# A graph layer on one core: edges turned by VectorE in blocks of 32x32, own rows fetched in four transfers

## The chip, the cores and the metric

One core of a Trainium2 chip runs the whole layer in one launch. The metric is the device time of one execution in microseconds; three executions of the kernel before gave 17,978.58, 17,993.09 and 18,013.70 us, a median of 17,993.09 us. The engines of the core work side by side, each through its own list of instructions in order: PE (TensorE), DVE (VectorE), ACT (ScalarE), POOL (GpSimd) and SP (SyncE, which here only starts transfers). They wait for one another through semaphores.

## The reference

50,000 nodes have 160 features each: 64 scalars and 32 vectors of three. There are 1,650,000 edges, sorted by their target `dst`; 50,000 of them lead from a node to itself. Each edge has four numbers.

```python
s, v = x[:, :64], x[:, 64:].reshape(n, 32, 3)
ss, vv = s[src], v[src]
e0, e1 = sh[:, 0:1], sh[:, 1:4]
dot = einsum('eui,ei->eu', vv, e1)
out0 = C0 * (ss * e0 @ W1 + dot * INV3 @ W2)
p3 = (ss @ W3)[:, :, None] * e1[:, None, :] * INV3
p4 = einsum('eui,uw->ewi', vv * e0[:, :, None], W4) * INV3
p5 = einsum('eui,uw->ewi', cross(vv, e1[:, None, :]), W5) * INV6
m = concatenate([out0, (C1 * (p3 + p4 + p5)).reshape(-1, 96)], axis=1)
m_agg = segment_sum(m, dst, n)
h = (m_agg times Ws and Wv)
x = layernorm(x + (x + relu(h)))
```

The messages are linear in x[src] and in the four numbers of the edge. So the kernel sums, for each node and each of the four numbers k, `attr[e, k] * x[src[e]]` over the node's edges, and applies one matrix of 4 x 160 rows by 160 columns, made of all weights, to each node afterwards.

## The kernel before

**Units.** 128 edges are a unit, 6 units (768 edges) a group, 2 groups a pair, 20 groups (10 pairs) a load. There are 2,087 groups, 1,044 pairs and 105 loads. As edges are sorted, the targets of a group lie within 32 consecutive nodes (`W`).

**A pair.** For each of its 12 units POOL starts one indirect transfer (`gather`, L349): 128 rows of x, picked by the indices in `si`, go to `xg`. There are four buffers of `xg`, so POOL may be 4 x 12 gathers ahead of PE. VectorE makes the weights of the sums (`spread`): `hot` (L358) marks which of 32 nodes each edge belongs to, `ha` (L361) multiplies it by the four numbers in `pk`. PE multiplies `ha` by `xg`, unit by unit, into `ps` (L386; each product is two weight loads and two matmuls in the profile). VectorE turns `ps` in blocks of 32x32 (L398, `turn_sums`) and adds each group's result to `ring` at the group's place (L405). The ring holds 768 nodes; a segment is 512 nodes, and at a segment's first group the part that reached past the last segment is carried over (L402). The order in VectorE's and PE's lists is that of the main loop: in pair p, after the second product `turn_sums` of pair p-1 is emitted, after the fourth `spread` of pair p+1, and tasks from a queue are worked off in between.

**Blocks.** When the last group that can touch a block of 128 nodes has been summed (`last_of`), its block is due: 391 in all, 2 or 3 pairs apart. Two pairs later PE multiplies the ring by the matrix (L704, `phb`), then VectorE adds x (y, L182, which waits for `phb`), makes the statistics and the normed row, and SP sends it out.

**Placing a load.** SP loads 120 units with a unit on each partition. `place`, four pairs later, turns them so that an edge lies on each partition: a product with a matrix of ones (L320) spreads each group's first target, from `first` (L318) to `baseB` (L322); PE transposes sources and targets into PSUM (L326, L327) and the four numbers into `pk` (L331); VectorE makes the indices `si` (L334) and the offsets `rel` (L337). `aim` turns the groups' first targets into places in the ring.

**Own edges.** All edges behind the first 76,800 are first packed (`pack`): VectorE takes the edges from a node to itself out of rows of 790 edges, SP writes the rest to `edges` and the four numbers of the own edges to `selves`, both in DRAM, by two transfers for each of 1,994 rows. Loads behind the first five read from `edges`, 24 bytes an edge. The own edges' share is put in when a segment begins: `ask_own`, six pairs ahead, loads x of 256 nodes to all four quarters of the partitions (`xr`, 640 KB) and the shares (`sr`, single numbers); `set_own`, two pairs ahead, multiplies them (L689) and turns the product into the ring (L693).

SP's list holds all loads and stores in the order of emission; a transfer that must wait holds those behind it.

Of the kernel before, what the change touches and what calls it, by code (L numbers as in the profile page):

```python
# [39 lines left out]
F32 = mybir.dt.float32  # L40
I32 = mybir.dt.int32
# [3 lines left out]
ALU = mybir.AluOpType  # L45
# [57 lines left out]
def tile_gnn_resnorm(ctx: ExitStack, tc: tile.TileContext, x, src, dst, attr, W1, W2, W3, W4, W5, Ws, Wv, out, n_edges):  # L103
# [123 lines left out]
    with tc.tile_pool(name="once", bufs=1) as once, tc.tile_pool(name="raw", bufs=2) as rawp, \  # L227
# [17 lines left out]
        nc.vector.tensor_copy(slotsP, slots)  # L245

# [3 lines left out]
        def load(s):  # L250

            g0 = s * SG
            n = (min(NG, g0 + SG) - g0) * G
            if g0 >= NH:
                p0 = g0 * G * P - EH
                r6 = rawp.tile([P, P, 2 + NK], F32, name="r6")
                dq.dma_start(r6[:n].rearrange("u p c -> u (p c)"),
                             edges[0, p0 * (2 + NK):(p0 + n * P) * (2 + NK)].rearrange("(u q) -> u q", u=n))
                return s, n, None, r6[:n, :, 0], r6[:n, :, 1], r6[:n, :, 2:]
            e = slice(g0 * G * P, (g0 * G + n) * P)  # L260
            ri = rawp.tile([P, 2, P], I32, name="ri")
            ra = rawp.tile([P, P, NK], F32, name="ra")
            dq.dma_start(ri[:n, 0, :], src1[e].rearrange("(u p) o -> u (p o)", p=P))
            dq.dma_start(ri[:n, 1, :], dst1[e].rearrange("(u p) o -> u (p o)", p=P))
            dq.dma_start(ra[:n].rearrange("u p k -> u (p k)"), attr[e].rearrange("(u p) k -> u (p k)", p=P))
            return s, n, ri, None, None, ra[:n]

        def cast(loaded):
            s, n, ri, sf, df, af = loaded
            if ri is not None:  # L270
                rf = rawp.tile([P, 2, P], F32, name="rf")
                begun.append(nc.scalar.copy(rf[:n], ri[:n]))
                sf, df = rf[:n, 0, :], rf[:n, 1, :]
            return s, n, sf, df, af
# [37 lines left out]
        def place(cast_):  # L312

            s, n, sf, df, af = cast_
            ng = n // G

            first = idxp.tile([P, SG], F32, name="first")
            nc.vector.tensor_scalar(first[:n], starts[:n], df[:, 0:1], None, op0=ALU.mult)  # L318
            yield 1
            nc.tensor.matmul(bank[:, 3, :ng], ones[:n], first[:n, :ng], start=True, stop=True)  # L320
            baseB = idxp.tile([P, SG], F32, name="baseB")
            nc.vector.tensor_scalar(baseB[:, :ng], bank[:, 3, :ng], float(N - 1), None, op0=ALU.min)  # L322
            aim(s, ng, baseB)
            yield 1
            pi = bank[:, 1:3, :]
            nc.tensor.transpose(pi[:, 0, :n], sf, ident[:n, :n])  # L326
            nc.tensor.transpose(pi[:, 1, :n], df, ident[:n, :n])  # L327
            yield 1.5
            pk = psK.tile([P, NK, P], F32, name="pk")
            for k in range(NK):  # L330
                begun.append(nc.tensor.transpose(pk[:, k, :n], af[:, :, k], ident[:n, :n]))  # L331
                yield 0.75
            si = idxp.tile([P, P], I32, name="si")
            nc.vector.tensor_scalar(si[:, :n], pi[:, 0, :n], 0.0, float(N - 1), op0=ALU.max, op1=ALU.min)  # L334
            rel = idxp.tile([P, P], F32, name="rel")

            nc.vector.scalar_tensor_tensor(  # L337
                rel[:, :n].rearrange("p (g j) -> p g j", j=G), pi[:, 1, :n].rearrange("p (g j) -> p g j", j=G),
                float(N - 1), baseB[:, :ng].unsqueeze(2).to_broadcast([P, ng, G]),
                op0=ALU.min, op1=ALU.subtract)  # L340
            nc.vector.tensor_reduce(extremes[:, 0, s:s + 1], rel[:, :n], axis=AX.X, op=ALU.min)
            begun.append(nc.vector.tensor_reduce(extremes[:, 1, s:s + 1], rel[:, :n], axis=AX.X, op=ALU.max))
            placed[s] = si, rel, pk
# [50 lines left out]
        def turn_sums(p, ps):  # L394

            s, g, ng = pairs[p]
            at = sump.tile([P, PG, ND, W], F32, name="sums")
            nc.vector.transpose(at[:, :ng], ps[:, :ng].rearrange("p g (b f) -> p g b f", f=FB))  # L398
            for i in range(ng):
                k = seg_of[g + i]  # L400
                if k and g + i == first_of[k]:
                    nc.vector.tensor_tensor(ring[k][:, :, :TW - S], ring[k][:, :, :TW - S], ring[k - 1][:, :, S:],  # L402
                                            op=ALU.add)
                here = ring[k][:, :, ds(find(g + i), W)]
                nc.vector.tensor_tensor(here, here, at[:, i], op=ALU.add)  # L405
# [255 lines left out]
        def ask_own(k, bs, got):  # L661
# [7 lines left out]
            xr = ownp.tile([P, BP * P // W, D], F32, name="xr")  # L669
            sr = ownp.tile([P, BP * P // W], F32, name="sr")  # L670
            xs = x[n0:n1, :].rearrange("(w q) d -> w (q d)", q=nq).unsqueeze(0).to_broadcast([NK, m, nq * D])
            ss = selves[0, n0 * NK:n1 * NK].rearrange("(w q k) -> k w q", q=nq, k=NK)
            with nc.allow_non_contiguous_dma(reason="one number of each node"):
                if m == W:
                    dq.dma_start(xr[:, :nq].rearrange("p q d -> p (q d)"), xs)
                    dq.dma_start(sr[:, :nq], ss)
                else:
                    nc.vector.memset(xr[:, :nq], 0.0)
                    nc.vector.memset(sr[:, :nq], 0.0)
                    for k_ in range(NK):  # L680
                        r = slice(k_ * W, k_ * W + m)
                        dq.dma_start(xr[r, :nq].rearrange("p q d -> p (q d)"), xs[k_])
                        dq.dma_start(sr[r, :nq], ss[k_])
            got.extend((xr, sr, nq))

        def set_own(k, bs, got):

            xr, sr, nq = got
            nc.vector.tensor_tensor(xr[:, :nq], xr[:, :nq], sr[:, :nq].unsqueeze(2).to_broadcast([P, nq, D]), op=ALU.mult)  # L689
# [25 lines left out]
        starts = once.tile([P, SG], F32, name="starts")  # L715
        nc.gpsimd.iota(starts, pattern=[[G, SG]], base=0, channel_multiplier=-1, allow_small_or_imprecise_dtypes=True)
        nc.vector.tensor_scalar(starts, starts, 0.0, None, op0=ALU.is_equal)
# [9 lines left out]
        nc.vector.memset(limit, float(KM))  # L727
        none = once.tile([P, 1], I32, name="none")
# [98 lines left out]

        packs, due = [], []
        for i in range(npacks):

            first = next(s for s in range(NH // SG, NSC)
                         if min(NG, (s + 1) * SG) * G * P - EH > row_start(i * RP)[0][0])
            own = next((k for k in range(NSEG) if min((k + 1) * S, N) > row_start(i * RP)[1][0] and own_blocks(k)), NSEG - 1)
            due.append(min((first - 1) * per - 1, first_of[own] // PG - 7))
# [4 lines left out]
        for k in range(1, NSEG):  # L839
            p = first_of[k] // PG  # L840
            after_pair(max(p - 3, START), begin_segment, k)
            for bs in own_blocks(k):
                got = []
                after_pair(p - 6, ask_own, k, bs, got)
# [8 lines left out]
        for p, (s, g, ng) in enumerate(pairs):  # L853
            if p % per == 0 and s + 1 < NSC:
                end = min(NG, (s + 2) * SG) * G * P - EH
# [200 lines left out]
```

## Time and profile before

| what | value |
|---|---|
| median of three executions | 17,993.09 us |
| the profiled execution | 18,022.17 us |
| its span, first to last instruction | 18,020.0 us |
| mean granted clock of TensorE | 0.625 |
| POOL busy | 12,137.8 us (67%) |
| DVE busy | 7,032.6 us (39%) |
| PE busy | 6,879.0 us (38%) |
| DMA queue of POOL, share of 16 engines | 23.7% |
| DMA queue of SP, share of 16 engines | 6.1% |

A row of the page's groups reads: line, engine, operation, what it writes and reads, how often; then busy time in us and the mean of one in ns; then how long the engine was idle just before such instructions, and what ended most of that. "issue" means that the engine waited for nothing that the profile shows, "remote" that a semaphore ended the wait whose sender the profile can't name. A row of waits reads: who waited, for whom, us in total, how many times, the longest. A row of the timeline reads: start in us, duration in us, engine, line, operation, and in brackets the idle time before.

### The profile page before, as it was taken

The numbers are of one execution on the slowest core, as the hardware profiler recorded it, in microseconds if no ns is written. First come the engines' busy times: TensorE is split into PE (matmuls) and PEld (weight loads), VectorE is DVE, ScalarE is ACT, GpSimd is POOL, SyncE is SP. The second block draws the span as 40 slices with busy tenths as digits, with TensorE's granted clock in tenths as the row PEclk, the third lists the DMA queues.
The fourth block names the chain that finished last, engine by engine and source line by source line (L and its number), as shares of the span: only waits on it lengthen the run. The fifth ranks groups of instructions, "written<-read, shape, count | busy, mean of one in ns | idle before, by whom it ended". The sixth has DMA issues, their size and how long they took to land. (4 is left out here: it accounts for less than half of the span.)

```text
span 18020.0 us, 99721 instructions
## 1 busy us (share of the span) xinstructions
PE 6879.0 (38%) x29811; PEld 6014.7 (33%) x29812; DVE 7032.6 (39%) x11269; ACT 227.8 (1%) x479; POOL 12137.8 (67%) x12535
## 2 busy tenths in 40 slices
PE   3333334343333333333333333334333333333333
PEld 3333333333333333333333333333333333333333
DVE  4343443434434343443433434344343433434332
ACT  0000000000000000000000000000000000000000
POOL 6666666666666666666666666666666666666666
PEclk6666666666666666666666666666666666666666
DMA  2222323232232322323223232322323223232222
GB/s 71 74 69 72 80 71 81 69 82 72 73 79 70 83 71 73 79 69 81 72 72 79 70 79 72 82 69 72 80 70 82 69 73 80 69 79 72 73 72 63
DMA packets 961715, 1337.18 MB, mean 74 GB/s; under 512 B 411739, under 2 KB 716048, under 8 KB 957182
## 3 DMA queue, kind: packets, MB, share of 16 engines
q0 software_dynamic: 601056, 1026.60, 23.7%
q1 hardware_dynamic: 358674, 302.87, 6.1%
q8 instruction: 238, 3.90, 0.1%
q14 instruction: 307, 2.51, 0.0%
q10 hardware_dynamic: 1440, 1.29, 0.0%
HBM read 1258.50 MB, written 71.40 MB: 74 GB/s over the span
## 5 line engine op out<-in xcount | busy, mean ns | idle before, releaser
L349 POOL DMA_INDIRECT xg<-in_x,si x12522 | 12134.1, 969 | 5859.5 <-issue 3666.1
L386 PE MATMUL ps<-xg,ha 128*128 128x160 f32 x25044 | 6255.4, 383 | 9081.8 <-issue 8146.9
L386 PEld LDWEIGHTS ps<-xg,ha 128*128 128x128 f32 x25044 | 5171.1, 254 | 9859.0 <-issue 8902.6
L398 DVE STREAM_TRANSPOSE sums<-ps 128x320 f32<-128x320 f32 x1044 | 529.7, 507 | 6341.5 <-remote 4050.5
L361 DVE TENSOR_TENSOR ha<-hot,pk 128x1536 f32<-128x1536 f32 x1044 | 1830.2, 1753 | 35.8
L182 DVE SCALAR_TENSOR_TENSOR y<-phb,xt 128x160 f32<-128x160 f32 x391 | 125.6, 321 | 3508.3 <-PE ps L386 1623.2
L704 PE MATMUL phb<-BWk,ring 128*128 128x160 f32 (+1 forms) x3910 | 1181.7, 388 | 454.0 <-issue 452.9
L704 PEld LDWEIGHTS phb<-BWk,ring 128*128 128x128 f32 (+1 forms) x3910 | 925.6, 266 | 470.0 <-issue 469.5
L405 DVE TENSOR_TENSOR ring<-ring,sums 128x160 f32 x2087 | 683.1, 327 | 309.7 <-issue 224.2
L358 DVE TENSOR_TENSOR hot<-bank,rel 128x384 f32<-128x384 f32 x1044 | 572.4, 548 | 107.0 <-remote 70.5
L693 DVE STREAM_TRANSPOSE ring<-xr 128x1280 f32<-128x1280 f32 x188 | 466.1, 2479 | 6.5
L566 DVE COPY_PREDICATED prow<-marks,prow 128x2370 f32<-128x2370 int32 (+8 forms) x160 | 445.4, 2784 | 1.1
L320 PE MATMUL bank<-first,ones 120*128 120x20 f32 (+1 forms) x210 | 59.4, 365 | 815.1 <-DVE first L318 573.0
L320 PEld LDWEIGHTS bank<-first,ones 120*128 120x128 f32 (+1 forms) x210 | 49.8, 292 | 853.6 <-DVE first L318 597.5
L191 ACT ACTIVATE rstd<-mv,eps_t 128x1 f32<-128x1 f32 x391 | 115.2, 295 | 17061.4 <-DVE st L184 5415.1
L326 PE MATMUL bank<-ident,r 120*128 120x120 f32 x100 | 46.2, 462 | 703.1 <-issue 361.0
L566 DVE COPY_PREDICATED pra<-marks,pra 128x1580 f32<-128x1580 int32 (+8 forms) x160 | 306.5, 1915 | 0.0
L689 DVE TENSOR_TENSOR xr<-xr,sr 128x1280 f32<-128x1280 f32 x188 | 277.0, 1473 | 57.4 <-DMA sr<-selves 35.9
L326 PEld LDWEIGHTS bank<-ident,r 120*128 120x128 f32 x100 | 21.1, 211 | 727.4 <-issue 369.7
L196 DVE TENSOR_SCALAR o<-y,mv,rstd 128x160 f32<-128x160 f32 x391 | 146.1, 374 | 19.6 <-issue 3.7
L402 DVE TENSOR_TENSOR ring<-ring 128x1280 f32<-128x1280 f32 x97 | 143.0, 1474 | 1.8
L331 PE MATMUL pk<-ident,r 120*128 120x120 f32 (+1 forms) x400 | 139.5, 400 | 0.0
(349 smaller groups left out, 2156.2 us busy)
## 6 DMA issues: line engine op xcount, KB each, us to landing
xg<-in_x,si POOLq DMA_INDIRECT x12522
xr<-in_x SPq DMA_DIRECT2D x187, 640.0 KB
edges<-prow SPq DMA_DIRECT2D x1994, 18.5 KB
r<-edges SPq DMA_DIRECT2D x99, 360.0 KB
selves<-mine SPq DMA_DIRECT2D x1992, 0.5 KB
xt<-in_x SPq DMA_DIRECT2D x195, 160.0 KB
out<-o SPq DMA_DIRECT2D x195, 160.0 KB
pra<-in_attr SPq DMA_DIRECT2D x15, 1580.0 KB
```

The costliest lines, as they stand in the source:

```text
L196: nc.vector.tensor_scalar(o[:n], y[:n], mv[:n, 0:1], rstd[:n], op0=ALU.subtract, op1=ALU.mult)
L349: nc.gpsimd.indirect_dma_start(out=xg[:, j, :], out_offset=None, in_=x, in_offset=bass.IndirectOffsetOnAxis(ap=placed[0][:, u + j:u + j + ...
L358: nc.vector.tensor_tensor(hot[:, :n], slotsP[:, 0:W].unsqueeze(1).to_broadcast([P, n, W]), rel[:, u:u + n].unsqueeze(2).to_broadcast([P, n ...
L361: nc.vector.tensor_tensor(ha[:, :n], hot[:, :n].unsqueeze(2).to_broadcast([P, n, NK, W]), pk[:, :, u:u + n].rearrange("p k u -> p u k").un ...
L386: mm = nc.tensor.matmul(ps[:, j // G, :], ha[:, j].rearrange("p k w -> p (k w)"), xr, start=j % G == 0, stop=j % G == G - 1)
L398: nc.vector.transpose(at[:, :ng], ps[:, :ng].rearrange("p g (b f) -> p g b f", f=FB))
L402: nc.vector.tensor_tensor(ring[k][:, :, :TW - S], ring[k][:, :, :TW - S], ring[k - 1][:, :, S:], op=ALU.add)
L405: nc.vector.tensor_tensor(here, here, at[:, i], op=ALU.add)
L566: nc.vector.copy_predicated(what[:n, a:e], mi[:, r].unsqueeze(2).to_broadcast([n, e - a, what.shape[2]]), what[:n, a + d:e + d])
L689: nc.vector.tensor_tensor(xr[:, :nq], xr[:, :nq], sr[:, :nq].unsqueeze(2).to_broadcast([P, nq, D]), op=ALU.mult)
L693: nc.vector.transpose(ring[k][:, :, c0:c0 + nq * W].rearrange("p b (w q) -> p q b w", q=nq), xr[:, :nq].rearrange("p q (b f) -> p q b f", ...
L704: wrote("misc", nc.tensor.matmul(ph[:nb], ring[k][:, i, c0:c0 + nb], BWk[:, i, :], start=i == 0, stop=i == ND - 1))
```

## The change

Placing does without PE. A load is always 128 units, and it lands so that each quarter of 32 partitions holds 32 edges of every unit; VectorE's transposes of 32x32 blocks then put an edge on each partition. The group's first targets are loaded separately, one number for each of 32 groups, in all four quarters, and are turned by VectorE as well. The own rows come in four transfers, one for each quarter, each emitted a pair later than the one before; the shares come as whole rows of four numbers, which VectorE masks by the quarter (`shareP`) and sums into PSUM (`sumP`). The carry-over between segments is cut to the columns that can have been reached, and done in five instructions. `reach` tells how far a load reads, for the order of packing.

```diff
+        shareP, sumP = bank[:, 3, 64:64 + NK], bank[:, 3, 96:96 + BP * P // W]
         def load(s):
             g0 = s * SG
-            n = (min(NG, g0 + SG) - g0) * G
+            ng = min(NG, g0 + SG) - g0
+            u0, f0 = (g0 * G, g0) if s + 1 < NSC else ((g0 + ng) * G - P, g0 + ng - W)
+            at = (g0 * G - u0, g0 - f0, ng)
+            def fetch(to, what, c):
+                rows = what.rearrange("(u i q) -> i u q", u=P, i=NK)
+                dq.dma_start(to, rows)
+            def fetch_first(to, what, c):
+                firsts = what.rearrange("(g q) -> g q", g=W)[:, 0:1]
+                with nc.allow_non_contiguous_dma(reason="one number of each group"):
+                    dq.dma_start(to, firsts.unsqueeze(0).to_broadcast([NK, W, 1]))
             if g0 >= NH:
-                p0 = g0 * G * P - EH
-                r6 = rawp.tile([P, P, 2 + NK], F32, name="r6")
-                dq.dma_start(r6[:n].rearrange("u p c -> u (p c)"),
-                             edges[0, p0 * (2 + NK):(p0 + n * P) * (2 + NK)].rearrange("(u q) -> u q", u=n))
-                return s, n, None, r6[:n, :, 0], r6[:n, :, 1], r6[:n, :, 2:]
...
+                r6 = rawp.tile([P, NK, W, C], F32, name="r6")
+                fd = rawp.tile([P, 1], F32, name="fd")
+                fetch_first(fd, edges[0, q0 * C + 1:(q0 + W * G * P) * C + 1], C)
+                fetch(r6.rearrange("p b e c -> p b (e c)"), edges[0, p0 * C:(p0 + P * P) * C], C)
...
         def place(cast_):
-            first = idxp.tile([P, SG], F32, name="first")
-            nc.vector.tensor_scalar(first[:n], starts[:n], df[:, 0:1], None, op0=ALU.mult)
-            yield 1
-            nc.tensor.matmul(bank[:, 3, :ng], ones[:n], first[:n, :ng], start=True, stop=True)
-            baseB = idxp.tile([P, SG], F32, name="baseB")
-            nc.vector.tensor_scalar(baseB[:, :ng], bank[:, 3, :ng], float(N - 1), None, op0=ALU.min)
-            aim(s, ng, baseB)
+            baseB = idxp.tile([P, W], F32, name="baseB")
+            nc.vector.transpose(baseB, fd.to_broadcast([P, W]))
+            base = baseB[:, f0:f0 + ng]
+            nc.vector.tensor_scalar(base, base, float(N - 1), None, op0=ALU.min)
+            aim(s, ng, base)
             yield 1
             pi = bank[:, 1:3, :]
-            nc.tensor.transpose(pi[:, 0, :n], sf, ident[:n, :n])
-            nc.tensor.transpose(pi[:, 1, :n], df, ident[:n, :n])
-            yield 1.5
+            nc.vector.transpose(pi.rearrange("p c (l b) -> p c b l", b=NK), ef)
+            yield 1
             pk = psK.tile([P, NK, P], F32, name="pk")
-            for k in range(NK):
-                begun.append(nc.tensor.transpose(pk[:, k, :n], af[:, :, k], ident[:n, :n]))
-                yield 0.75
+            begun.append(nc.vector.transpose(pk.rearrange("p k (l b) -> p k b l", b=NK), af.rearrange("p b e k -> p k b e")))
+            yield 1
...
         def turn_sums(p, ps):
-                    nc.vector.tensor_tensor(ring[k][:, :, :TW - S], ring[k][:, :, :TW - S], ring[k - 1][:, :, S:],
-                                            op=ALU.add)
+                    past = max(high[first_of[k - 1]:first_of[k]]) + W - k * S
+                    for b in range(ND):
+                        nc.vector.tensor_tensor(ring[k][:, b, :past], ring[k][:, b, :past], ring[k - 1][:, b, S:S + past],
+                                                op=ALU.add)
...
-        def ask_own(k, bs, got):
+        def ask_own(k, bs, got, part):
-            xs = x[n0:n1, :].rearrange("(w q) d -> w (q d)", q=nq).unsqueeze(0).to_broadcast([NK, m, nq * D])
-            ss = selves[0, n0 * NK:n1 * NK].rearrange("(w q k) -> k w q", q=nq, k=NK)
-                    dq.dma_start(xr[:, :nq].rearrange("p q d -> p (q d)"), xs)
-                    dq.dma_start(sr[:, :nq], ss)
...
+            r = slice(part * W, part * W + m)
+            dq.dma_start(xr[r, :nq].rearrange("p q d -> p (q d)"), x[n0:n1, :].rearrange("(w q) d -> w (q d)", q=nq))
+            shares = selves[0, n0 * NK:n1 * NK].rearrange("(w f) -> w f", w=m)
...
+            elif part == 0:
+                dq.dma_start(sa[:, :nq].rearrange("p q k -> p (q k)"),
+                                shares.unsqueeze(0).to_broadcast([NK, W, nq * NK]))
         def set_own(k, bs, got):
-            xr, sr, nq = got
-            nc.vector.tensor_tensor(xr[:, :nq], xr[:, :nq], sr[:, :nq].unsqueeze(2).to_broadcast([P, nq, D]), op=ALU.mult)
+            xr, sa, nq = got
+            nc.vector.tensor_tensor(sa[:, :nq], sa[:, :nq], shareP.unsqueeze(1).to_broadcast([P, nq, NK]), op=ALU.mult)
+            nc.vector.tensor_reduce(sumP[:, :nq], sa[:, :nq], axis=AX.X, op=ALU.add)
+            nc.vector.tensor_tensor(xr[:, :nq], xr[:, :nq], sumP[:, :nq].unsqueeze(2).to_broadcast([P, nq, D]), op=ALU.mult)
...
-            due.append(min((first - 1) * per - 1, first_of[own] // PG - 7))
+            due.append(min((first - 1) * per - 1, first_of[own] // PG - 9))
...
-                after_pair(p - 6, ask_own, k, bs, got)
+                for part in range(NK):
+                    after_pair(p - 8 + part, ask_own, k, bs, got, part)
                 after_pair(p - 2, set_own, k, bs, got)
```

## The prediction

> **What bounds the kernel now.** First the page's share of each engine, then its costliest group.
>
> ```profile
> PE 6879.0 (38%) x29811; PEld 6014.7 (33%) x29812; DVE 7032.6 (39%) x11269; ACT 227.8 (1%) x479; POOL 12137.8 (67%) x12535
> ...
> L349 POOL DMA_INDIRECT xg<-in_x,si x12522 | 12134.1, 969 | 5859.5 <-issue 3666.1
> ```
>
> No engine is full, but POOL does one thing from end to end: 12522 gathers. Their busy time and their idle time add up to 12134.1 + 5859.5 = 17993.6 us of the 18020 us span. So the question is what each gather costs and what stands between two of them. The waits of POOL alone:
>
> ```profile
> POOL xg L349 <- issue: 3666.1, 11991, 2.1
> POOL xg L349 <- PE ps L386: 1224.7, 236, 46.9
> POOL xg L349 <- remote: 875.2, 223, 7.0
> ```
>
> The first row is POOL's own issue time, 3666.1 / 11991 = 0.306 us each. The other rows are real waits. I went through all gathers in the trace: the median one takes 0.949 us and the median gap is 0.305 us, so the floor is 12522 x 1.254 = 15,702 us. Gathers longer than 1.0 us (428) hold 261 us more than the median, and gaps over 0.5 us (442) hold 2,037 us. With 22 us after the last gather and 8 before the first, less rounding, this is the span. The change can win from the 261 and the 2,037, and from nothing else. The timeline shows the waits:
>
> ```profile
> 8002.04 0.95 POOL L349 DMA_INDIRECT xg<-in_x,si  x1 [0.30 <-issue]
> 8003.12 0.28 PEld L386 LDWEIGHTS ps<-xg,ha 128*128 128x128 f32 x1 [2.51 <-issue]
> 8004.52 0.43 PE L386 MATMUL ps<-xg,ha 128*128 128x160 f32 x1 [2.37 <-issue]
> 8005.22 0.29 PEld L386 LDWEIGHTS ps<-xg,ha 128*128 128x128 f32 x1 [1.82 <-issue]
> ...
> 8006.64 0.33 DVE L182 SCALAR_TENSOR_TENSOR y<-phb,xt 128x160 f32<-128x160 f32 x1 [29.56 <-remote]
> ...
> 8009.25 0.95 POOL L349 DMA_INDIRECT xg<-in_x,si  x1 [6.26 <-remote]
> ```
>
> Before the wait PE crawls, one instruction each 0.7 or 1.4 us; VectorE has stood 29.56 us at y (L182), which needs PE's phb; then POOL, out of free xg buffers, stands 6.26 us and all go on. Of the 442 waits 426 are at the first gather of a pair, and most are 3.5 to 6.5 us long. Counted against the pairs at which `last_of` starts the 391 blocks, 295 of 390 intervals between blocks hold exactly one wait, 27 none, the others more: about one wait for each block, and 442 - 391 = 51 besides. By the pair's place in its load, pairs 1 to 8 hold 199 us each, pair 9 (four pairs behind `place`) 342 us, pair 0 only 102 us. So blocks pace the waits and `place` adds some.
>
> The long gathers have another cause:
>
> ```profile
> 8014.27 0.94 POOL L349 DMA_INDIRECT xg<-in_x,si  x1 [0.30 <-issue]
> 8015.31 1.48 DVE L689 TENSOR_TENSOR xr<-xr,sr 128x1280 f32<-128x1280 f32 x1
> ...
> 8015.51 2.10 POOL L349 DMA_INDIRECT xg<-in_x,si  x1 [0.30 <-issue]
> ...
> 8020.71 2.50 DVE L693 STREAM_TRANSPOSE ring<-xr 128x1280 f32<-128x1280 f32 x1
> ...
> 8021.81 0.95 POOL L349 DMA_INDIRECT xg<-in_x,si  x1 [0.30 <-issue]
> ```
>
> A gather beside L689 takes 2.10 us, one beside the transpose L693 the usual 0.95. Over the run: with only L689 beside them, 30 of 37 gathers are long, with only L402 26 of 28, with only L693 0 of 189, with only L361 0 of 782. L689 and L402 read two SBUF operands; L361 is as long but has pk in PSUM:
>
> ```profile
> L361 DVE TENSOR_TENSOR ha<-hot,pk 128x1536 f32<-128x1536 f32 x1044 | 1830.2, 1753 | 35.8
> ...
> L405 DVE TENSOR_TENSOR ring<-ring,sums 128x160 f32 x2087 | 683.1, 327 | 309.7 <-issue 224.2
> ...
> L320 PE MATMUL bank<-first,ones 120*128 120x20 f32 (+1 forms) x210 | 59.4, 365 | 815.1 <-DVE first L318 573.0
> ...
> L689 DVE TENSOR_TENSOR xr<-xr,sr 128x1280 f32<-128x1280 f32 x188 | 277.0, 1473 | 57.4 <-DMA sr<-selves 35.9
> ...
> L402 DVE TENSOR_TENSOR ring<-ring 128x1280 f32<-128x1280 f32 x97 | 143.0, 1474 | 1.8
> ```
>
> **The change, part by part.** *Own rows.* The product in `set_own` now reads xr and the sums in PSUM, the form of L361. All long gathers that touch L689 hold 180 us over the median. Bounds: 0 (it blocks as before) and -180; I take -180, because 782 gathers beside an operand in PSUM show no delay. Its own time stays: 1753/1536 x 1280 = 1461 ns against 1473. Two small operations come on (32 elements; nearest rows 0.17 to 0.28 us): 188 x 0.45 = 85 us of VectorE, hidden under its 61% idle time; uncovered it would be 85.
>
> [...]
>
> *The carry-over* (L402) becomes five adds of 133 to 256 columns each, 215 on average. 51 us of long gathers touch it. The nearest short row is L405, also two SBUF operands, 0.327 us: 2087 of them leave some 15 us in long gathers. Bounds: 0 and -51; I take -45, by that row.
>
> *Placing.* For each of 105 loads PE loses 1 matmul with ones (L320) and 6 transposes (L326, L327, L331), 735 in all of about 15,250, and with them the relay first (DVE) -> L320 (PE) -> baseB (DVE) -> L326 (PE) -> si (DVE). PE idles 815 us before L320 and 703 before L326, VectorE 267 before baseB and 107 before si; none of it is a loss by itself, only where POOL feels it. Bounds for POOL: pairs 9 and 0 together hold 342 + 102 - 2 x 199 = 45 us above the level; 51 waits beyond one per block, at 2,037 / 442 = 4.6 us, are 235. I take -140, the middle. VectorE gets three transposes instead: 512 and 256 elements at 1.6 to 1.9 ns (L398: 508 ns for 320; L693: 2479 for 1280) and a small one, 1.4 to 1.7 us, less 0.22 for first: some 150 us over 105 loads, hidden in the same idle time.
>
> *Transfers.* SP issues xr four times for each pair of blocks, at p-8 to p-5 instead of once at p-6: 748 issues for 187; shares come as 128 pieces of 128 B instead of 1024 of 4 B; a load comes as 512 rows of 768 B instead of 120 of 3,072 B, with one more transfer of 128 single numbers. Today the second xr holds SP for 13.8 us (8413.64, SP's own timeline), and edges, selves, xt and out stand behind it; that goes. 561 + 105 more transfers on 5,200 of SP are 13%, on all with the gathers 4%. Bytes hardly change. Bounds on the waits: -50 to +200 (a tenth of 2,037); I take +20, as y waits for xt only 242 us in all.
>
> *New waits.* VectorE stands at the first transpose of `place` until the load has landed, and at `set_own` until the fourth part has; behind it stand sums, hot and ha, so PE and at last POOL. The load is asked for about four pairs (60 us) ahead, the last part three pairs (45 us).
>
> Sum: 18,020 - 180 - 45 - 140 + 20 = 17,675 us. The profiled execution took 18,022 against a median of 17,993, 29 us less: I predict **17,650**.
>
> **The rivals.** *The waits take the gain back* (chance 0.11): PE's crawl, not POOL, sets the period, and a POOL that is no longer held at L689 waits longer. For it: 295 intervals of one wait per block. Against it: the waits are 4 or 6 us whatever came before, so they come on top. Time: 17,993 - 20 of placing, some 17,970. 0.2% (36 us) is what a measurement of this kernel tells from no change.
>
> *The relay is the trigger* (0.12): VectorE's long stand at y starts with `place` having put PE late. For it: 815 us of PE idle at L320. Against it: pairs 1 to 8 of a load wait as much as others. With a third of the waits gone: 17,993 - 225 - 680 = 17,090.
>
> *Late loads* (0.13; slower): place, the transposes at L341 and L347. 512 + 128 pieces behind stores and xr parts on SP's queue land after VectorE's turn. POOL feels it only when VectorE is more than about 48 gathers (60 us) behind. From 365 / 105 = 3.5 us of POOL wait per load it is a loss; at 6 us: 17,993 - 365 + 630 = 18,260. Against it: SP has no stall of 13.8 us any more, and all 16 DMA engines are 30% busy.
>
> *It does not do what it says*: that the order of VectorE leaves the gathers blocked as before; part of the first rival.
>
> **How the numbers follow.** The forecast (17,500 to 17,800) gets 0.50, a weaker gain (17,800 to 17,950) 0.14. The range runs from 17,330, a little over half of the way to the second rival, to 17,970, the parts with port gain and waits a tenth up: it leaves out most of the second and third rival, 0.2. The likeliest case's own range is 17,530 (235 for placing) to 17,800. Faster: 0.50 + 0.14 + 0.12 = 0.76 and 0.02 of the first rival, 0.78; same 0.09; slower 0.13.
>
> **What would show it.** Gathers beside the product with sums in PSUM at 0.95 us, the total of long gathers near 40 us; some 400 gaps over 0.5 us with 1,850 to 1,950 us; no peak at pair 9; idle time of VectorE before its new transposes small. The prediction is wrong if the gathers stay long, if waits keep or pass 2,037 us, or if they fall far below one for each block.

## The result and the profile after

The kernel after takes 17,932.06 us (median of 7; 17,915.07 to 17,953.16) against 17,991.28 us (7 runs of before): a ratio of 0.9966, interval 0.9957 to 0.9976. It is faster by 0.34%, where 2% was forecast. The profiled execution has a span of 17,930.3 us, 90 us less than before's 18,020.0.

The page's shares of the engines, its costliest group, and the new product:

```profile
PE 7015.8 (39%) x28971; PEld 6090.6 (34%) x28972; DVE 7265.0 (41%) x12244; ACT 228.6 (1%) x484; POOL 11920.4 (66%) x12535
...
L368 POOL DMA_INDIRECT xg<-in_x,si x12522 | 11916.7, 952 | 5988.1 <-issue 3652.2
...
L712 DVE TENSOR_TENSOR xr<-xr,bank 128x1280 f32<-128x1280 f32 x188 | 278.9, 1483 | 138.8 <-DMA xr<-in_x 63.5
```

POOL is busy 217 us less (12134.1 to 11916.7), but its idle time is 129 us more (5859.5 to 5988.1). The view of POOL's waits:

```profile
POOL xg L368 <- issue: 3652.2, 11917, 2.6
POOL xg L368 <- PE ps L405: 1445.4, 272, 39.3
POOL xg L368 <- remote: 812.0, 209, 6.8
```

The row of issue is as before (3652.2 / 11917 = 0.306 us each). The row of PE grew from 1,224.7 to 1,445.4 us. Counted over all gathers as in the prediction, the floor is the same (median 0.949 us, gap 0.305 us). What a long gather takes above the median I call a *hold*: the holds sum to 40.6 us (261 before). What a gap over 0.5 us has above the median gap I call a *wait*: the waits sum to 2,161 us in 485 gaps (2,037 in 442). So -220 and +124, and +4 because the first gather starts at 12.0 us (8.1 before): -92, the 90 us of the span. The holds went as forecast, and more than half of what they gave came back as waits. The timeline shows that the cause of the holds is gone:

```profile
8163.97 1.49 DVE L712 TENSOR_TENSOR xr<-xr,bank 128x1280 f32<-128x1280 f32 x1
...
8164.65 0.95 POOL L368 DMA_INDIRECT xg<-in_x,si  x1 [0.30 <-issue]
...
8165.90 0.95 POOL L368 DMA_INDIRECT xg<-in_x,si  x1 [0.31 <-issue]
```

The gather that starts within the product takes 0.95 us; beside L689 it took 2.10.

One thing must be known to read the rest. The experiments ran in series, each on one chip beside its own runs of before, and the median of before itself was 17,991 to 18,153 us in some series and 15,975 to 15,993 us in others, once one and once the other on the very same chip. I call them *waiting* and *quiet* series; ratios are taken within a series only.

| series | before, us | kernels |
|---|---|---|
| 1, waiting | 17,991.28 | the kernel after |
| 2, waiting | 18,001.46 | x1 to x4 |
| 3, waiting | 18,002.53 | x5 to x8 |
| 4, quiet | 15,974.83 | x9 to x12 |
| 5, quiet | 15,992.51 | y1 to y3 |
| 6, waiting, chip of series 5 | 18,153.48 | z1 |
| 7, quiet, chip of series 5 | 15,990.69 | w1, w2 |

### The profile page after: what moved, and what is told of

Read it like the earlier page. It is cut to its first block, busy times and chain, and to the rows that moved or that the text cites. A ratio compares the mean times of both kernels' runs of the same rounds, so it can differ in the third digit from the quotient of the medians.

```text
span 17930.3 us, 99703 instructions
## 1 busy us (share of the span) xinstructions
PE 7015.8 (39%) x28971; PEld 6090.6 (34%) x28972; DVE 7265.0 (41%) x12244; ACT 228.6 (1%) x484; POOL 11920.4 (66%) x12535
## 3 DMA queue, kind: packets, MB, share of 16 engines
q14 instruction: 321, 2.63, 0.0%
## 5 line engine op out<-in xcount | busy, mean ns | idle before, releaser
L368 POOL DMA_INDIRECT xg<-in_x,si x12522 | 11916.7, 952 | 5988.1 <-issue 3652.2
L405 PE MATMUL ps<-xg,ha 128*128 128x160 f32 x25044 | 6529.4, 393 | 10583.3 <-issue 9697.2
L405 PEld LDWEIGHTS ps<-xg,ha 128*128 128x128 f32 x25044 | 5395.4, 261 | 11509.9 <-issue 10642.6
L417 DVE STREAM_TRANSPOSE sums<-ps 128x320 f32<-128x320 f32 x1044 | 526.7, 505 | 4709.6 <-remote 3280.4
L182 DVE SCALAR_TENSOR_TENSOR y<-phb,xt 128x160 f32<-128x160 f32 x391 | 126.0, 322 | 5136.0 <-PE ps L405 3505.8
L712 DVE TENSOR_TENSOR xr<-xr,bank 128x1280 f32<-128x1280 f32 x188 | 278.9, 1483 | 138.8 <-DMA xr<-in_x 63.5
L423 DVE TENSOR_TENSOR ring<-ring 128x196 f32<-128x196 f32 (+20 forms) x485 | 148.9, 372 | 1.8
L184 DVE BATCH_NORM_STATS2 st<-y 128x6 f32<-128x160 f32 x391 | 128.1, 328 | 13.4
L674 DVE MEMSET ring<- 128x1280 f32 (+1 forms) x98 | 119.3, 1218 | 22.8 <-issue 22.8
L584 DVE COPY_PREDICATED_SCALAR hit<-marks,none 128x395 int32 (+8 forms) x160 | 105.2, 658 | 5.7
L350 DVE STREAM_TRANSPOSE pk<-r 128x512 f32<-128x512 f32 x100 | 104.0, 1040 | 0.0
L585 DVE COPY_PREDICATED hit<-marks,pri 128x395 int32<-128x395 int32 (+8 forms) x160 | 95.6, 598 | 6.2 <-issue 0.7
```

The source lines that it names most:

```text
L368: nc.gpsimd.indirect_dma_start(out=xg[:, j, :], out_offset=None, in_=x, in_offset=bass.IndirectOffsetOnAxis(ap=placed[0][:, u + j:u + j + ...
L405: mm = nc.tensor.matmul(ps[:, j // G, :], ha[:, j].rearrange("p k w -> p (k w)"), xr, start=j % G == 0, stop=j % G == G - 1)
L423: nc.vector.tensor_tensor(ring[k][:, b, :past], ring[k][:, b, :past], ring[k - 1][:, b, S:S + past], op=ALU.add)
L712: nc.vector.tensor_tensor(xr[:, :nq], xr[:, :nq], sumP[:, :nq].unsqueeze(2).to_broadcast([P, nq, D]), op=ALU.mult)
```

## The experiments

**The parts one by one (series 2).** In x1 only the product of before gets its sums from PSUM; no other part of the change is in it.

```diff
+        sumP = bank[:, 3, 96:96 + BP * P // W]
...
+            nc.vector.tensor_copy(sumP[:, :nq], sr[:, :nq])
-            ... xr[:, :nq], sr[:, :nq].unsqueeze(2) ...
+            ... xr[:, :nq], sumP[:, :nq].unsqueeze(2) ...
```

> The kernel before, with one edit: the shares are copied into PSUM, and the product of the own rows reads them there. Theory A (POOL that is held less runs into PE's delay more often, so waits take back part of the port's gain): long gathers fall by some 160 to 180 us, but POOL's waits over 0.5 us rise above 2,037 us by 60 to 120, the time is 60 to 120 us below the kernel before. Theory B (the new placing, or the new transfers, add the waits): the waits stay at 2,037 +- 30 us, the time is 160 to 180 us below, near 17,815 us.

18,008.4 us, ratio 1.0008 (0.9998 to 1.0017). Long gathers fell from 261 to 88 us; the waits rose from 2,037 to 2,184 us (463). POOL's waits in x1:

```profile
POOL xg L350 <- PE ps L387: 1290.7, 248, 47.9
POOL xg L350 <- remote: 1010.1, 250, 7.2
```

Both rows lie above before's 1,224.7 and 875.2. Of 173 us of holds won, 147 came back as waits, with no edit but the one that ends the hold. (The trace of before is of series 1; by the medians of series 2 the whole of it came back.) That is the whole riddle in one kernel.

In x2 the change's placing stands alone: own rows, shares, carry-over and due times are those of before.

```diff
-                    for b in range(ND):
-                        nc.vector.tensor_tensor(ring[k][:, b, :past], ...)
+                    nc.vector.tensor_tensor(ring[k][:, :, :TW - S], ...)
... (own rows and shares as in before)
-                for part in range(NK):
-                    after_pair(p - 8 + part, ask_own, k, bs, got, part)
+                after_pair(p - 6, ask_own, k, bs, got)
```

> The kernel after, with own rows, shares and carry-over of the kernel before: only the placing by VectorE and its loads. Theory A: waits within 50 us of 2,037 or somewhat below, long gathers as before (250 us), the time within 60 us of the kernel before. Theory B with placing as the cause: waits at 2,130 us or more, the time 60 to 150 us above the kernel before. My prediction had 140 us less.

17,982.41 us, ratio 0.9988 (0.9979 to 0.9998). Holds 257.5 us, waits 1,989 us (422). Pair 9 of a load has 208 us of waits where it had 342: the peak is gone, but the total fell by 48 us only.

In x3 the kernel after fetches the own rows in one transfer again, six pairs ahead.

```diff
-            dq.dma_start(xr[r, :nq]..., x[n0:n1, :]...)
...
+            elif part == 0:
+                dq.dma_start(xr[:, :nq]..., rows.unsqueeze(0).to_broadcast([NK, W, nq * D]))
-                    after_pair(p - 8 + part, ask_own, k, bs, got, part)
+                    after_pair(p - 6, ask_own, k, bs, got, part)
```

> The kernel after, with the own rows of 256 nodes in one transfer of 640 KB six pairs ahead instead of four of 160 KB. Theory B with the transfers as the cause: waits fall from 2,161 us to some 2,050, the time is near 17,830 us. Theory A: the waits stay within 40 us of 2,161 and the time within 40 us of the kernel after.

17,942.66 us, ratio 0.9968 (0.9957 to 0.998), waits 2,202 us: no different from after. The four transfers are worth nothing here.

In x4 VectorE takes y two pairs after the block's products in place of at once.

```diff
-            for d, f in ((2, do_block), (3, do_root), (4, do_store), (6, do_send)):
+            for d, f in ((2, do_block), (4, do_norm), (5, do_root), (6, do_store), (8, do_send)):
```

> The kernel after, with y and what follows it two pairs later than the block's matmuls, so that VectorE meets y when the matmuls should long be done. If VectorE's stand at y is what paces the waits (about one for each block), the 5,136 us that VectorE is idle before y fall below 1,000, POOL's waits fall from 2,161 us by a third or more, and the time below 17,250 us. If PE's late signals pace them wherever VectorE happens to wait, VectorE stands as long before the transposes of the sums instead, and the time stays within 100 us of the kernel after.

17,921.62 us, ratio 0.9961 (0.9947 to 0.9975), waits 2,160 us (480). VectorE's stand at y moved to the transpose of the sums: there (L417) it waits 9,277.7 us for PE and "remote" together, where the kernel after has 4,457.0, and y is no longer among the eleven longest rows of waits (3,505.8 us for PE in the kernel after). POOL's waits stayed. So the block's y does not pace them.

**The usual suspects (series 3).** x5 gives the rows a fifth buffer (and `ops` two for three, for the room).

```diff
-            ... tc.tile_pool(name="rows", bufs=4) as rowp, \
-            tc.tile_pool(name="ops", bufs=3) as op, ...
+            ... tc.tile_pool(name="rows", bufs=5) as rowp, \
+            tc.tile_pool(name="ops", bufs=2) as op, ...
```

> The kernel after with five buffers of xg instead of four (and two of hot and ha instead of three, for the room). Theory A1 (PE's late signals come free only while POOL stands still, a fixed rest for each stretch of PE's work): POOL runs 12 gathers further before it stands, the waits become fewer, but the rest needed stays, the time falls by 0 to 300 us from 17,932. Theory A2 (the four buffers are simply too few for a delay of 20 to 35 us): most waits of 4 to 6 us vanish, the time falls below 16,900 us.

18,012.65 us, ratio 1.0006 (0.9996 to 1.0015), waits 2,225 us (486). More lead did not help: the ratio is 0.4% above after's. As `ops` lost a buffer in the same edit, the 0.4% cannot be put down to the lead alone.

x6 leaves out four of the five products of each block.

```diff
-            for i in range(ND):
+            for i in range(1):
```

> The kernel after without four of the five products of each block (the output lacks four fifths of the sums): PE has 11% fewer instructions, VectorE, POOL and the transfers have the same. If the number of PE's instructions sets how often its signals come late, POOL's waits fall by 200 us or more, the time to 17,730 us or below. If the gathers' own traffic sets it, whatever PE does, the time stays within 60 us of 17,932.

17,946.29 us, ratio 0.9968 (0.9955 to 0.998), waits 2,186 us (449). A tenth less of TensorE's matmuls (25,843 for 28,971) changed nothing.

x7 leaves out the products of every second unit.

```diff
+                if j % 2:
+                    yield ps
+                    continue
...
-                                      start=j % G == 0, stop=j % G == G - 1)
+                                      start=j % G == 0, stop=j % G == G - 2)
```

> The kernel after without the products of every second unit (the sums lack half of the edges); all 12,522 gathers stay. PE has 43% fewer instructions and signals. If their number sets the waits, these fall below 700 us and the time below 16,500 us. If the gathers' traffic alone delays PE, the waits stay above 1,700 us and the time above 17,500 us.

18,050.72 us, ratio 1.0025 (1.0015 to 1.0035). Its POOL:

```profile
POOL xg L368 <- remote: 1969.7, 356, 11.6
POOL xg L368 <- PE ps L408: 399.0, 31, 45.1
```

The waits sum to 2,308 us (405), more than in any run before it, though TensorE is busy 3,974 us in place of 7,016 and the crawl of one instruction each 0.7 or 1.4 us can't be found in the trace any more: PE's idle time under "issue" before the group products comes in 837 waits of 13.8 us on average, where the kernel after has 4,621 of 2.1 us.

x8 keeps all products but takes rows and `ha` as float32r. In the profile each of the 12,522 group products then has one matmul in place of two (16,449 matmuls in all for 28,971).

```diff
-            xg = rowp.tile([P, PG * G, D], F32, name="xg")
+            xg = rowp.tile([P, PG * G, D], mybir.dt.float32r, name="xg")
-            ha = op.tile([P, PG * G, NK, W], F32, name="ha")
+            ha = op.tile([P, PG * G, NK, W], mybir.dt.float32r, name="ha")
```

> The kernel after with xg and ha as float32r (the gather casts, VectorE writes the weights so), so that a unit's product needs one weight load and one matmul if the chip runs it in one pass, and nothing is left out. If PE's number of instructions sets the waits, they fall below 900 us and the time below 16,700 us, the largest gain of all; if the gather with a cast costs POOL more than 0.949 us each, each 0.01 us more costs 125 us. If PE's number has no part in it, the time is 17,932 us plus what the cast costs.

18,055.1 us, ratio 1.0033 (1.0022 to 1.0044), no crawl (788 waits under "issue" of 13.7 us on average), waits 2,364 us (430). So neither the amount of TensorE's work nor its crawl as such makes the waits, and one gather in each 1.43 to 1.44 us came out of every one of these kernels.

**The gathers themselves (series 4, which turned out quiet).** x9 lets all group products read one fixed tile, so nobody reads what is gathered and POOL waits for no TensorE.

```diff
-                mm = nc.tensor.matmul(ps[:, j // G, :], ha[:, j]..., xr,
+                mm = nc.tensor.matmul(ps[:, j // G, :], ha[:, j]..., hold,
...
+        hold = once.tile([P, D], F32, name="hold")
+        nc.sync.dma_start(hold, x[0:P, :])
```

> The kernel after, with every matmul of the groups (L405) reading one fixed tile of 128 rows in place of the gathered ones; the gathers are all issued as before but nobody reads them, so that the sums are not those of the edges. GpSimd then waits for no TensorE, and TensorE for no gather; a row buffer is free when its own earlier gathers have landed. Theory 'the gathers' own path': the 1.43 us per gather that all runs so far share (12,522 gathers in 17.93 to 18.06 ms) come from the gathers themselves, so 17,930 +- 80 us and over 1,900 us of waits (then put down to something else than PE). Rival 'the hand-over from TensorE': the waits go with the signal, under 500 us are left, and the time falls to 15,702 + some 600 = 16,300 +- 300 us.

15,753.15 us, ratio 0.9862 (0.9846 to 0.9879). Against 18,000 this would have looked like a proof that TensorE's signals are late. But before took 15,974.83 us beside it, so that the run only says: without waits the gathers need 12,522 x 1.251 us.

x10 gathers 64 rows in place of 128 and contracts over 64.

```diff
-                    out=xg[:, j, :], ...
+                    out=xg[:P // 2, j, :], ...
... (indices and weights cut to P // 2 in the same way)
```

> The kernel after, with each gather fetching 64 rows for 64 partitions in place of 128, and the matmuls contracting over those 64; half of the edges are left out. The same number of gathers, of matmuls, of signals. Theory 'the gathers' own path, by rows': both the burst (0.949 us) and the 1.43 us on average fall, by a third or more, to under 13,000 us. Rival 'by instructions or signals': GpSimd's own 0.949 us may fall, but the time stays within 3% of 17,930, with waits of 2,100 us and whatever GpSimd saved on top.

15,227.36 us, ratio 0.9533 (0.9517 to 0.9549). The mean gather fell from 949 ns (x9) to 906 ns: half the rows save 43 ns, and 12,522 x 0.043 = 538 us accounts for the 526 us between x10 and x9. In these two runs the price of a gather hardly depends on its rows: half of them take 95% of the time.

x11 leaves out every sixth gather (its product takes the rows before it).

```diff
+                if j % 6 == 5:
+                    continue
...
-            return [xg[:, j, :] for j in range(n)]
+            return [xg[:, j - (j % 6 == 5), :] for j in range(n)]
```

> The kernel after, with every sixth gather left out (its matmul reads the row tile before it, so that a sixth of the edges is taken with other rows); 10,435 gathers in place of 12,522, all else the same. Theory 'a price for each gather': 10,435 x 1.43 = 14,950 +- 150 us. Rival 'waits per pair': 10,435 x 1.254 + the 2,160 us of waits that 1,044 pairs have = 15,250 +- 100 us. Rival 'the other engines' work sets a pair's 17.2 us': 17,800 us or more.

13,144.44 us, ratio 0.8229 (0.8215 to 0.8243): 10,435 x 1.251 = 13,054 and 52 us of long gathers and gaps besides, with some 35 us at both ends. Below all three expectations, because the waits that each had put in were absent.

x12 adds three holding operations behind each product of before.

```diff
+            for _ in range(3):
+                nc.vector.tensor_tensor(xr[:, :nq], xr[:, :nq], xr[:, :nq], op=ALU.max)
```

> The kernel before, with three more operations of VectorE behind each of its 188 products (the greater of the product and itself, both operands in SBUF, 128 x 1280), which change no value. The 188 products held GpSimd for some 173 us (long gathers 261 us against 88 with one operand in PSUM); 564 more of the kind should add some 520 us of long gathers. Theory 'holds and waits trade': the waits fall from 2,037 to some 1,550 us, and the time rises by less than 100 us. Rival 'holds add up', on which the prediction was built: +450 to +600 us, 18,450 to 18,600.

16,127.93 us, ratio 1.0096 (1.0079 to 1.0113): +153 us. The holds sum to 437 us; against the 261 of before's trace (of series 1, since before has no trace of a quiet series) that is +176, a third of what I expected of 564 such operations. But what there is of holds comes out in the time: in a quiet series holds add up.

**The change in a quiet series (series 5).** The kernel after itself:

> The kernel after, unchanged, beside before on whatever chip this call gets. Theory 'waits belong to the chip, holds add where there are none': on a chip on which before takes some 15,975 us, the 220 us of long gathers saved come out whole, 15,760 +- 40 us, a ratio of 0.984 to 0.989, with under 100 us of waits over 0.5 us; on a chip on which before takes some 18,000 us the ratio is 0.996 to 0.998 as before. Rival 'the change gives the gain back by its own waits': on any chip a ratio of 0.995 to 0.999, so 15,895 us or more where before takes 15,975.

15,765.82 us against 15,992.51: ratio 0.986 (0.9843 to 0.9876), 227 us faster. Its page:

```profile
L368 POOL DMA_INDIRECT xg<-in_x,si x12522 | 11890.7, 950 | 3848.7 <-issue 3522.5
L405 PE MATMUL ps<-xg,ha 128*128 128x160 f32 x25044 | 10077.0, 513 | 5027.1 <-DMA xg<-in_x,si 4930.6
```

and POOL's waits:

```profile
POOL xg L368 <- issue: 3522.5, 11549, 1.5
POOL xg L368 <- PE ps L405: 232.5, 763, 0.3
POOL xg L368 <- DMA xg<-in_x,si: 76.5, 184, 2.1
```

The same program, instruction for instruction, has 2,140 us less idle time on POOL. The longest wait for PE is 0.3 us, which is a gap like any other. Waits sum to 23 us (31), holds to 31 us. TensorE's idle time is put down to the landing of the gathers, where the same line in series 1 has "issue":

```profile
L405 PE MATMUL ps<-xg,ha 128*128 128x160 f32 x25044 | 6529.4, 393 | 10583.3 <-issue 9697.2
```

The first matmul on a row tile starts 1.66 us (median) after POOL has ended its gather; in series 1 it is 35.1 us for this kernel and 34.4 us for before. The expectation was right in its numbers and wrong in its word "chip", as series 6 showed on the same one.

> Fixed rows once more (every group matmul reads one fixed tile, the gathered rows are read by nobody, so the sums are not those of the edges). On a chip on which before takes some 15,975 us: 15,750 again. On a chip on which it takes some 18,000: theory 'the gathers' own path is slower there' 17,930 +- 80 us; rival 'TensorE's signals come late there' 16,300 us or less, with under 500 us of waits.

15,774.28 us, ratio 0.9864 (0.9847 to 0.988): a repeat of x9, which leaves the question open.

> The kernel before with three more operations behind each product, once more. On the chip without waits they made 176 us more of long gathers (437 against 261) and 153 us more of time. On a chip on which before takes some 18,000 us: theory 'holds and waits trade' says long gathers up by some 175 us, waits down by 100 us or more from 2,037, and the time up by less than 75 us; rival 'holds add up' says the time up by 130 to 180 us and the waits unchanged.

16,146.41 us, ratio 1.0096 (1.0079 to 1.0113): +154 us with 442 us of holds, a repeat of x12.

**Fixed rows in a waiting series (series 6).**

> Fixed rows a third time (every group matmul reads one fixed tile, so the sums are not those of the edges), for a chip on which before takes some 18,000 us. There: theory 'the gathers' own path is slower' 17,930 +- 80 us; rival 'TensorE's signals come late' 16,300 us or less, with under 500 us of GpSimd's waits. On a chip on which before takes some 15,980 us it can only repeat 15,760 +- 20.

22,252.67 us against 18,153.48, ratio 1.2258 (1.2238 to 1.2279): neither theory. The waits of POOL, and of PE:

```profile
POOL xg L368 <- DVE rel L356: 6531.1, 105, 99.6
POOL xg L368 <- issue: 3787.4, 12405, 2.3
```

```profile
PE ps L405 <- issue: 10141.4, 4319, 28.2
PE ps L405 <- DVE ha L380: 4036.0, 531, 80.8
PE phb L727 <- issue: 1052.8, 488, 3.1
```

POOL, which no TensorE holds any more, runs to the end of the placed load, and stands there, once a load, for up to 99.6 us: `place` is late, since VectorE is behind TensorE, and TensorE is far behind the gathers. Three windows of z1, one before such a stand, the stand (10420.7 to 10492.8 us) and one behind it, with the busy time and number of instructions of PE, PEld, DVE, ACT and POOL:

```profile
10281.00:10420.70 139.70, 21.07 (x53) 14.80 (x53) 7.22 (x12) 0.00 (x0) 105.89 (x112) 0.51 0.31 87
10420.70:10492.80 72.10, 34.05 (x173) 31.86 (x173) 49.05 (x92) 7.46 (x8) 0.02 (x1) 0.69 0.21 53
10492.80:10642.50 149.70, 33.45 (x122) 27.11 (x121) 26.41 (x49) 0.29 (x1) 113.47 (x120) 0.55 0.26 70
```

and the first window of the same kernel in series 4, at the same times:

```profile
10281.00:10420.70 139.70, 47.33 (x262) 45.39 (x260) 57.37 (x100) 0.89 (x3) 105.68 (x112) 0.66 0.33 79
```

Beside the same 112 gathers TensorE makes 262 matmuls in the quiet series and 53 in the waiting one; while POOL stands, it makes 173 in half the time. Over all of z1 it is 0.74 matmuls a us while gathers go out, and 2.63 in POOL's stands. The timeline of z1 just before the stand:

```profile
10416.03 0.95 POOL L368 DMA_INDIRECT xg<-in_x,si  x1 [0.30 <-issue]
10416.82 0.29 PEld L405 LDWEIGHTS ps<-hold,ha 128*128 128x128 f32 x1 [2.52 <-issue]
10417.28 0.95 POOL L368 DMA_INDIRECT xg<-in_x,si  x1 [0.30 <-issue]
10418.22 0.43 PE L405 MATMUL ps<-hold,ha 128*128 128x160 f32 x1 [2.38 <-issue]
10418.53 0.95 POOL L368 DMA_INDIRECT xg<-in_x,si  x1 [0.30 <-issue]
10419.61 0.29 PEld L405 LDWEIGHTS ps<-hold,ha 128*128 128x128 f32 x1 [2.50 <-issue]
```

A weight load or a matmul each 1.4 us, with rows that no gather has to bring. In a waiting series, then, TensorE is slow while gathers go out, and catches up after POOL has stopped.

The catching up comes late. In z1's 103 stands of over 20 us TensorE starts 0.36 matmuls a us in the last 10 us before the stand, no more than 0.52 in its first 10 us, and 4.1 between 30 and 40 us into it. In the kernel after (424 waits of over 3 us) it starts 0.61 a us from 12 to 2 us before the gathers go on, 1.47 in the last 2 us, and 3.2 from 4 to 12 us behind the wait, while gathers go out again. So the gathers stop first, and TensorE runs fast some time later; why it takes that long no run shows.

The four row buffers bound POOL's lead, and with it TensorE's backlog; z1 has no such bound but the load, and lost 4,100 us. That the longer lead is what cost them is argued, not tested.

**A shorter lead (series 7, quiet again).** Three row buffers, then two, in place of four:

```diff
-            ... tc.tile_pool(name="rows", bufs=4) as rowp, \
+            ... tc.tile_pool(name="rows", bufs=3) as rowp, \
```

> The kernel after with three buffers of rows in place of four: GpSimd can be 36 gathers ahead of TensorE in place of 48. Theory 'the lead costs' (five buffers 18,012 us, four 17,932, no limit but the load 22,250, each beside a before of 18,000 to 18,150): a ratio of 0.990 to 0.995, 17,820 to 17,910 us where before takes 18,000. Rival 'the quiet time is a fixed need of TensorE': 0.996 to 0.998, as with four. Where before takes some 15,980 us, TensorE is 1.3 us behind a gather's landing, so that three buffers change nothing: 0.986.

> The same with two buffers, 24 gathers of lead. Theory 'the lead costs': a ratio of 0.980 to 0.990 where before takes 18,000 us or more. Rival 'a fixed need': 0.996 to 0.998, or above 1 where the shorter lead makes GpSimd wait for TensorE's ordinary lag. Where before takes some 15,980 us: 0.986 to 0.990.

15,766.5 us, ratio 0.986 (0.9843 to 0.9876), and 15,769.0 us, ratio 0.9861 (0.9844 to 0.9877): the same as with four. (That TensorE is 1.3 us behind a gather's landing, as w1's expectation has it, no view here shows; measured in y1 are the 1.66 us from the end of POOL's gather.) Two buffers would do in a quiet series; whether they help in a waiting one is not known, as none of the series with them was one. No version that does the whole work of the layer beat the kernel after by more than the intervals.

## Why the prediction was wrong

*The sum's waits are the step that failed.* The prediction put -140 for the placing and +20 for the transfers on the waits, and let the two savings in holds stand beside them: 18,020 - 180 - 45 - 140 + 20. Measured: -220 in holds, as said, and +124 in waits where -120 stood. Its sentence against the first rival, "the waits are 4 or 6 us whatever came before, so they come on top", is what x1 refutes: with the hold alone removed, the waits rose by 147 us for the 173 us of holds, and the time stayed.

The first half of that sentence is largely true: 277 of before's 442 waits and 368 of after's 485 last 4 to 5 or 6 to 7 us. What it missed is that a hold puts off the next wait. The own-row products come in 94 pairs. From the end of a pair to POOL's next wait it is 31.3 us on average in before and 31.5 us in x2, where a pair has 1.96 and 1.93 us of holds; it is 19.6 us in x1, 20.2 us in the kernel after and 20.8 us in x3, whose products hold no gather (standard errors 0.9 to 1.4 us). Within before, the third of the pairs with the least hold (1.46 us) has its next wait after 23.8 us, the other two thirds after 34.8 and 35.5 us. So a hold acts like a short stand of POOL: it puts off the next wait by some 11.5 us. An estimate from this: 94 x 11.5 us, at 18,020 / 442 = 40.8 us from wait to wait, is 26 or 27 waits of 4.6 us, some 120 us; x1 gave back 147 us. Why POOL stands as often as it does in a waiting series stays open. It is not the blocks alone, as the prediction had it ("blocks pace the waits"): y1 has the same blocks and 23 us of waits.

What the prediction named as a sign of being wrong, waits that keep or pass 2,037 us, is what came. Its range holds 17,932 us, but only because its upper end, 17,970, let the waits rise by a tenth on account of the transfers; x3, with the own rows in one transfer, waits as long (2,202 us), and x2, with the new loads, less (1,989 us). So the range was met by luck.

*The holds were right, in cause and in size.* Beside L712 alone 0 of 95 gathers are long, and long gathers that touch the split carry-over (L423) have 13 us over the median (51 before). The forecast of -180 - 45 = -225 us is close to the 227 us that the change brings in a quiet series, where waits are few. One operand in PSUM ends the holds beside the own-row product: 30 of 37 gathers are long beside L689 alone, 0 of 95 beside L712 alone. By what VectorE holds POOL no run shows, so "port", the word of the prediction and of x1's expectation for this gain, is a name and no finding. Nor is the hold the same for all operations with both operands in SBUF. A gather beside the 1.48 us product takes 2.10 us; but x12's 564 operations, both inputs the same tile, made 176 us of holds, 0.31 us each: beside them alone 375 of 375 gathers take 1.22 us on average, beside L689 alone in the same run 42 gathers take 1.88.

*The placing* did remove the peak at pair 9 (342 us to 195 after, 208 in x2), but alone it is worth 48 us of waits and 0.12% of the time, not 140: most of the waits beyond one per block were no relay of `place`.

*The rivals.* "The waits take the gain back" (0.11) was nearest the truth in a waiting series: "a POOL that is no longer held at L689 waits longer" is what x1 shows, though its 17,970 us left too little of the gain (17,932). Its "PE's crawl, not POOL, sets the period" is not it: x7 and x8 have no crawl and wait more. "The relay is the trigger" falls with x2. "Late loads" did not come: VectorE stands 138.8 us before L712 in all (57.4 before L689), 63.5 of it for the rows, and x3 without the four transfers is no faster. The small terms held: the product takes 1,483 ns with its sums in PSUM against 1,473, so 10 ns more and 2 us in all.

## What to carry to other kernels

Two savings on one engine add up only if its waits don't depend on its pace (in x1 they did: 173 us of holds gone, 147 us of waits more): remove one hold alone, and look whether the engine's waits grow, before you sum. Where the others are slow while one engine issues gathers, as in the waiting series here (z1: 0.74 matmuls a us while gathers go out, 2.63 in POOL's stands), a pause of that engine is not all loss, as the others catch up behind it. And run the kernel before in every series: beside the 18,000 us of another series, x9 would have passed for a gain of 12%, and it was 1.4%.

## What the runs showed of the hardware

- The same program on the same chip takes 15,993 us in one series and 18,153 us in another (before), that is 1.28 and 1.45 us for each of its 12,522 gathers. What differs between the series is not known; the mean granted clock of TensorE does not tell them apart (the kernel after: 0.622 in the waiting series, 0.566 in the quiet one; fixed rows: 0.593 in z1, 0.663 in x9).
- In a waiting series the trace itself loses events: of the semaphores that VectorE alone raises in the kernel after, the instructions make 10,225 updates, and 4,925 are recorded in series 1, 10,225 in series 5; of all semaphores 54,901 updates against 252,568. All 11 traces of waiting series have 50,558 to 59,989 updates, all 9 of quiet ones 209,609 to 252,569. POOL's waits in the kernel after have 812.0 us under "remote" in series 1, and no such row among the seven longest in series 5, the last of which has 0.9 us. Whether the signals themselves are late in a waiting series, and whether the recording has a part in it, no run shows, as every execution has a recorded span.
- A gather of 64 rows (x10) takes 906 ns, one of 128 rows (x9) 949 ns; the 0.305 us between two gathers are the same.
- With 64 rows in each product (x10) TensorE was granted its full clock, 1.0, against 0.57 to 0.66 in the other kernels of that series.
